# Layer 0's x1 turned by DMA, and another order of products in a turn

## The chip, the cores and the metric

The kernel runs on 1 core of one Trainium2 chip. The metric is device time in microseconds (us) of the whole program; lower is better. Engines are named as in the profile: PE is TensorE (matmuls), PEld its weight loads, DVE is VectorE, ACT is ScalarE, POOL is GpSimd and SP is SyncE, which issues the DMAs.

## What is computed

There are 128 graphs of 64 nodes with 768 features, float32 throughout, and two layers. Each layer is `x = layernorm(x + layer(x, adj))`. Layer 0 is a graph attention of 12 heads with a gate; layer 1 is a masked self-attention of 6 heads.

```python
def _L0_gnn_ref(feat_in, adj, W, b, w_src, w_dst, H_w, H_b):
    h = jnp.einsum('bnd,ade->bane', feat_in, W)
    th = jnp.tanh(h)
    attn_src = jnp.einsum('bane,aeo->bano', th, w_src)
    attn_dst = jnp.einsum('bane,aeo->bano', th, w_dst)
    attn = attn_src + jnp.swapaxes(attn_dst, 2, 3)
    attn = jnp.where(attn >= 0, attn, LEAKY_ALPHA * attn)
    attn = jnp.where(~adj[:, None, :, :], jnp.float32(-999.0), attn)
    attn = jax.nn.softmax(attn, axis=-1)
    feat_out = jnp.einsum('banm,bame->bane', attn, h) + b
    feat_out = jax.nn.elu(heads_joined(feat_out))
    gate = jax.nn.sigmoid(feat_in @ H_w.T + H_b)
    return gate * feat_out + (1.0 - gate) * feat_in

def _L1_gnn_ref(seq_inputs, Wq, bq, Wk, bk, Wv, bv, Wf, bf, graph_mask):
    q, k, v = (_heads(seq_inputs @ w + c) for w, c in ((Wq, bq), (Wk, bk), (Wv, bv)))
    scores = jnp.einsum('bhqd,bhkd->bhqk', q, k) / np.sqrt(HEAD_SIZE)
    probs = jax.nn.softmax(scores + bias, axis=-1)      # bias: 0 or -9e15 by the mask
    return heads_joined(jnp.einsum('bhqk,bhkd->bhqd', probs, v)) @ Wf + bf
```

(`heads_joined` is shorthand for the swap of axes and the reshape.)

## The kernel before

The 8192 rows are worked in 32 pairs; a pair is two tiles of 128 rows, called tile 0 and tile 1. Every dense product of a pair is done by a scheme of seven block products instead of eight, so a product of a pair (`h`, the gate `g`, the values `v`, the output `o`) is a `Job` of seven steps. A name such as `h5` is product 5 of the job `h`; it is six matmuls of 128x128 by 128x384 (L275). Products 1, 2 and 4 read blocks of the transposed input itself; 6, 5, 7 and 3 read sums of blocks (`block_sums`, L245 to L248): product 5 reads the first sum, 6 the second, 7 the third, 3 the fourth. A job keeps one PSUM bank `y` from product 1 to product 4 or so, a bank `x` for product 2 and a bank `z` for products 5 and 3. Banks of `x` and `z` share the tag `z`, with three buffers; `y` has three, and a tag `m` two. What a product left in PSUM is taken out by `way_out` one step later, after the next product has been issued: for `h` and `v` by an ACT copy or a DVE addition (L837 to L839, L866 to L868), for the gate by DVE (L853 to L855).

The schedule is written out by hand (`manual_schedule`): engines run their instructions in the order of the program. Layer 0 is a loop of turns. A turn walks through a list of products (`TURN` in most turns), and at each position of the list a set of acts is issued after the product. In turn p, `n0` and `n1` are the tiles of the new pair p, whose `h` and gate are made and whose attention weights are prepared; `t0` and `t1` are the tiles of the old pair q = p - 1, whose attention, gating and layernorm are finished, and whose layer-1 values `v` are begun. Products called `u` are the rest of the values of the pair before that; `G` and `H` are a gate left over or an `h` begun early. The acts that the text speaks of:

- new pair: `products` (L873: tanh on ACT, two multiplications by the attention vectors on DVE and POOL), `terms` (L881: a sum over 64 on DVE, then a store `dstd` and two loads `dd` that spread one of the terms over the partitions), `with_bias` (L893: POOL, and two loads `hx` of half of h), `logits` (L913, DVE), `leaky` (L923, ACT), `masked` (L929 to L936, DVE), `exps` (L942, ACT);
- old pair: `probs_by_nodes` (six PE transposes, bank m, two ACT copies into `pT`), `attend` (L974: 48 small matmuls `av` in two banks m), `features` (L990, L991 on DVE, L998 on ACT), `gate_tanh` (L1054, L1055, ACT), `residual` (L1004, POOL), `elu1` and `gated` (L1009 to L1016, DVE), `stats` and `normed` (the layernorm, L321 to L331; the result x1 is stored to DRAM);
- then `by_features`: x1 is transposed by PE, six transposes a tile into bank m (L953, `x1Tp`), and ACT copies them into `x1T` (L954). `v_begins` and `v_sums` make the operands of `v` from `x1T` on DVE; `spill_features` stores `x1T` for layer 1, `spill_values` stores the finished v;
- for the next pair: `load_xT` and `x_sums`, four sums on POOL. From turn 2 until it is done `sum_weights` also builds sums of layer-1 weights, with POOL operations (L366) and small DMAs, one step at each position.

All DMAs are issued on SP, in order. The pools give three buffers to `h`, to the gate and to the small tiles, five to `work`, two to `x1`, `v` and `x`, one to `x1T`, `pT` and the sums.

The list of a usual turn and of the last one, and the acts that by_features belongs to:

```python
TURN = [
    "h1", "h2", "u4", "u3", "h6", "g1", "h5", "h7", "g2", "g6", "h4",
    "h3", "g5", "g7", "v1", "v2", "g4", "v6", "g3", "v5", "v7",
]
            was(8, do(by_features, t1), do(stats, t0))
            was(9, do(normed, t0))
            was(12, do(v_begins))
            was(15, lambda: v_sums[q][0](), lambda: v_sums[q][1](), do(spill_features, q))
            at(11, new, do(products, n1))
            was(11, do(by_features, t0))
```

Layer 1 turns its attention weights by DMA already: `split` copies the 16-bit halves of the words apart (ACT, L574), `send` stores them to DRAM, `turn` brings each half back transposed with `dma_start_transpose` (L584), `join` puts the halves together (ACT, L591).

Of the kernel before, what the change touches and what calls it, by code (L numbers as in the profile page):

```python
# [62 lines left out]
    7.5: 12, 0: 7, 1: 7, 2: 8, 3: 9, 4: 10, 5: 11, 6: 12, 7: 12, 8: 13, 9: 14, 11: 15, 12: 15, 15: 16, 16: 17, 19: 19,  # L63
# [31 lines left out]
    ["u4", "u3"]  # L95
    + [f"q{n}" for n in (0, 1, 2, 3, 4, 5, 6, 8, 7, 9, 10, 11, 12)]
    + ["v1", "v2", "v6", "q13", "v5", "v7", "q14", "v4", "v3"]
)
LAST_AT = {7.5: 8, 3: 3, 4: 4, 5: 5, 6: 6, 7: 7, 8: 9, 9: 10, 11: 12, 12: 13, 15: 15, 16: 17, 19: 18}
# [27 lines left out]
    "h1", "h2", "u4", "u3", "h6", "g1", "h5", "h7", "g2", "g6", "h4",  # L127
    "h3", "g5", "g7", "v1", "v2", "g4", "v6", "g3", "v5", "v7",
]

THIRD_AT = {pos: max(int(pos) - 2, 0) for pos in [*range(len(TURN)), 7.5]}
TURNS = {
    0: (FIRST, FIRST_AT, {}),
    1: (SECOND, SECOND_AT, SECOND_OLD),
    2: (TURN[2:], THIRD_AT, THIRD_AT),
}


@with_exitstack
def kernel(  # L140
# [41 lines left out]
    x1T_d = [dram.tile([P, KC, PAIR * P], F32, name=f"x1Td_{p}") for p in range(NP)]  # L182
    v_d = [dram.tile([P, D], F32, name=f"vd_{t}") for t in range(2 * NP)]
    dst_d = [dram.tile([P, H0], F32, name=f"dstd_{t}") for t in range(2 * NP)]

    halves_d = [dram.tile([2, GT, P, P], U16, name=f"halvesd_{i}") for i in range(3)]
# [40 lines left out]
    def all_of(steps):  # L227
        for s in steps:
            s()

# [263 lines left out]
    class Attention:  # L494
# [81 lines left out]
        def send(self):  # L576
            nc.sync.dma_start(
                out=halves_d[self.f].rearrange("h i p c -> p h i c"),
                in_=self.halves(self.scT_, False).rearrange("p h (i c) -> p h i c", c=P),
            )  # L580

        def turn(self):
            for h in range(2):
                nc.sync.dma_start_transpose(  # L584
                    out=self.halves(self.flat, False)[:, h],
                    in_=halves_d[self.f][h].rearrange("i p c -> (i p) c"),
                )
# [155 lines left out]
    with ExitStack() as ph, ExitStack() as ph_r:  # L743
# [21 lines left out]
        def sums_of(eng, pool, tag, t, name):  # L765
            return block_sums(
                eng,
                sum_tiles(pool, tag, P, name),
                t[:, :HK, :P],
                t[:, HK:, :P],  # L770
                t[:, :HK, P:],
                t[:, HK:, P:],
            )
# [17 lines left out]
        A[0], x_steps = sums_of(G, sbr, "sx", xTs[0], "x0")  # L791
# [78 lines left out]

        def products(t):

            h = st[t]["h"]  # L873
            th = sbr.tile([P, 2, D], F32, tag="th", name=f"th_{t}")
            S.activation(th[:, 1, :].rearrange("p (a e) -> p a e", e=E0), h[:, :, :E0], AF.Tanh)  # L875
            V.tensor_tensor(th[:, 0, :], th[:, 1, :], wsd[:, 0, :], ALU.mult)  # L876
            G.tensor_tensor(th[:, 1, :], th[:, 1, :], wsd[:, 1, :], ALU.mult)  # L877
            st[t]["th"] = th

        def terms(t):  # L880
# [5 lines left out]
            nc.sync.dma_start(out=dst_d[t], in_=sd[:, :H0])  # L886
            dd = work(f"dd_{t}")
            for g in range(2):
                nc.sync.dma_start(
# [137 lines left out]
        x1Ts, B = {}, {}  # L1027

        def by_features(t):
# [4 lines left out]
            for half in range(2):  # L1034
# [4 lines left out]
                )  # L1039

# [29 lines left out]
        def value_sums(q):  # L1070
            B[q], v_sums[q] = sums_of(V, sb, "sv", x1Ts[q], f"v{q}")

        def x_sums(p):
            operands, steps = sums_of(G, sbr, "sx", xTs[p], f"x{p}")
            all_of(steps)
            A.setdefault(p, {}).update(operands)

        def third_begins():
            x = xTs[2]
            A[2] = {1: x[:, :HK, :P], 2: x[:, HK:, :P]}  # L1080
            jobs["H"] = h_job(2)
# [13 lines left out]
        for p in range(NP + 1):  # L1095
# [3 lines left out]
            if new:  # L1099
                jobs["G"] = jobs.get("g")  # L1100
                jobs["h"], jobs["g"] = jobs["H"] if p == 2 else h_job(p), gate_job(p)
            plan = {}

            turn, of_new, of_old = TURNS.get(p, (TURN, {}, {})) if new else (LAST, {}, LAST_AT)

            def at(pos, ok, *acts, places=of_new):
                if ok:
                    plan.setdefault(places.get(pos, int(pos)), []).extend(acts)

            def was(pos, *acts):  # L1110
                at(pos, old, *acts, places=of_old)
# [4 lines left out]
            def v_begins():  # L1116
                value_sums(q)
                jobs["v"] = v_job(q)


            was(0, do(probs_by_nodes, t1))
            at(0, old, do(exps, t0), do(gate_tanh, t1), places={0: 6} if p == 1 else of_old)
            was(1, do(residual, t1))
            was(2, do(attend, t1), do(gate_tanh, t0))
            was(3, do(features, t1), do(probs_by_nodes, t0), do(residual, t0))
            was(4, do(elu1, t1), do(gated, t1))
            was(5, do(attend, t0), do(stats, t1))
            was(6, do(features, t0), do(normed, t1))
            was(7, do(elu1, t0))
            was(7.5, do(gated, t0))  # L1130
            was(8, do(by_features, t1), do(stats, t0))
            was(9, do(normed, t0))
            was(12, do(v_begins))
            was(15, lambda: v_sums[q][0](), lambda: v_sums[q][1](), do(spill_features, q))
            was(16, lambda: v_sums[q][2]())
            was(19, lambda: v_sums[q][3]())

            at(0, p + 1 < NP, do(load_xT, p + 1))
            at(3, new, lambda: adjs.__setitem__(p, load_adj(sb, 2 * p, PAIR, f"adj_{p}")))
            at(6, new, do(mask, p))  # L1140
            at(4, 0 <= p - 2 < NP, do(spill_values, p - 2))
            at(8, new, do(inputs, p))
            at(11, new, do(products, n1))
            was(11, do(by_features, t0))
            at(12, new, do(products, n0))
            at(13, new, do(terms, n1), do(with_bias, n1))
            at(14, new, do(terms, n0), do(with_bias, n0))
            at(15, new, do(plus_one, p))
            at(16, new, do(logits, n1))
            at(17, new, do(leaky, n1))  # L1150
            at(17, p + 1 < NP, do(x_sums, p + 1), places={17: 12} if p == 0 else of_new)
            at(18, new, do(masked, n1), do(logits, n0))
            at(19, new, do(exps, n1), do(leaky, n0))
            at(20, new, do(masked, n0))

            if p == NP - 1:

                at(2, True, do(load_wide, "q", wq, range(4)))
                at(8, True, do(load_wide, "q", wq, range(4, 8)))
                at(12, True, do(load_wide, "q", wq, range(8, NW)))  # L1160
                at(9, True, do(load_wide, "k", wk, range(4)))
                at(15, True, do(load_wide, "k", wk, range(4, 8)))
                at(18, True, queries_begin)
                at(20, True, do(load_wide, "k", wk, range(8, NW)), lambda: jobs["rows"].ready(2))
            if p == NP:
                flush()
                for act in plan.pop(0):
                    act()
# [6 lines left out]
            if p == 1:  # L1175
                at(14, True, third_begins, places={})
# [161 lines left out]
```

## Time and profile before

| | |
|---|---|
| median of 3 runs | 2906.42 us (2904.89 to 2909.09) |
| profiled execution | 2904.88 us, of which the span of instructions is 2903.1 us |
| granted TensorE clock | 0.997 |
| PE, DVE, ACT, POOL busy | 99%, 66%, 37%, 35% of the span |
| layer 0 | up to about 1535 us of the span |
| x1 transposes on PE (x1Tp) | 384 matmuls, 52.5 us busy |

The profile is of one execution. A line of the groups reads: source line, engine, operation, written tile <- read tiles, shapes, count, then busy us and mean ns of one, then the idle time of the engine just before them with what ended it. A line of the timeline starts with the time from the span's start and the length. In the row of 40 slices each digit is the busy share in tenths. PE's matmuls overlap, so the distance from one start to the next counts, not the length. "q" behind an engine's name (SPq) is its queue of DMA issues.

### The profile page before, as it was taken

To read this page: it belongs to the slowest core of one execution; us is meant where nothing else is said; L and a number is where in the kernel's file an instruction comes from. 1 tells how busy PE (TensorE), PEld (TensorE's weight loads), DVE (VectorE), ACT (ScalarE), POOL (GpSimd) and SP (SyncE) were. 2 spreads that over 40 slices of the span, in tenths; PEclk is the share of its full clock that TensorE was granted. 3 is DMA by queue.
4 is the path that set the end of the run, shared out by engine and by line. 5 is a ranking of instruction groups with operands and counts; after the bars stand their busy time and mean duration, and the time that the engine had idled before them with its cause. 6 is when DMAs were issued, how large, how long until landed. Compare 5 with 4: busy or idle time off the path is not lost.

```text
span 2903.1 us, 45587 instructions
## 1 busy us (share of the span) xinstructions
PE 2860.5 (99%) x17676; PEld 1965.3 (68%) x17676; DVE 1930.0 (66%) x3045; ACT 1060.0 (37%) x1896; POOL 1022.1 (35%) x857
## 2 busy tenths in 40 slices
PE   7999999999999999999999999999999999999998
PEld 4565665566665665666668777877777877777885
DVE  6888788888878888788863654554564454565445
ACT  2344444444444444444433312333312333312232
POOL 2434354443444444343352323332223332123321
PEclk9999999999999999999999999999999999999999
DMA  5344444444434343333353323333223333223332
GB/s 175 123 139 135 138 137 131 138 131 143 147 126 146 125 146 127 105 113 110 117 198 108 108 84 100 105 99 103 65 82 100 103 102 100 74 75 101 99 88 73
DMA packets 307864, 335.20 MB, mean 115 GB/s; under 512 B 146241, under 2 KB 234305, under 8 KB 307649
## 3 DMA queue, kind: packets, MB, share of 16 engines
q1 hardware_dynamic: 307648, 332.29, 36.3%
q8 instruction: 140, 2.29, 0.3%
q14 instruction: 76, 0.61, 0.1%
HBM read 188.26 MB, written 119.14 MB: 106 GB/s over the span
## 4 chain that ended last, share of the span: by engine, by line
PE 84%; DVE 9%; ACT 2%; DMA 2%; issue 2%; POOL 1%; SPq 1%; POOLq 0%; DVEq 0%; ACTq 0%
PE y_o L275 9%; PE z_k L444 8%; PE z_q L444 8%; PE y_h L275 7%; PE y_g L275 6%; PE y_v L275 6%; PE y_k L444 5%; PE y_q L444 5%; PE z_o L275 4%; PE z_h L275 4%; PE z_v L275 3%; PE z_g L275 3%; PE x_o L275 2%; PE x_g L275 2%; PE sp L518 2%
## 5 line engine op out<-in xcount | busy, mean ns | idle before, releaser
L542 ACT ACTIVATE sc<-sc 128x512 f32<-128x512 f32 x48 | 30.2, 629 | 735.1 <-DVE sc L539 735.1
L327 POOL TENSOR_TENSOR rs_b<-ve_b,minus_half 128x1 f32<-128x1 f32 x64 | 35.2, 550 | 645.0 <-DVE ve_b L325 576.9
L444 PE MATMUL z_q<-xs,w_wq 128*128 128x256 f32 x896 | 213.5, 381 | 0.3 <-POOL xs L408 0.3
L672 POOL TENSOR_TENSOR y<-y,bf_bc 128x768 f32<-128x768 f32 x64 | 125.2, 1978 | 247.1 <-DMA y<-x1d 247.1
L444 PE MATMUL z_k<-xs,hw_wk 128*128 128x256 f32 x840 | 200.0, 381 | 0.0
L459 DVE TENSOR_TENSOR qT<-qT,z_q 128x512 f32<-128x512 f32 x96 | 65.8, 686 | 200.7 <-PE z_q L444 200.6
L1004 POOL TENSOR_TENSOR x<-gate,x 128x768 f32<-128x768 f32 x64 | 117.5, 1837 | 229.7 <-ACT gate L1055 214.9
L408 POOL TENSOR_TENSOR xs<-r,r 128x512 f32<-128x512 f32 x112 | 155.0, 1400 | 96.3 <-PE z_k L444 62.9
L444 PEld LDWEIGHTS z_q<-xs,w_wq 128*128 128x128 f32 x896 | 168.7, 190 | 24.3 <-POOL xs L408 0.7
L877 POOL TENSOR_TENSOR th<-th,wsd 128x768 f32<-128x768 f32 x64 | 117.3, 1833 | 164.9 <-DVE th L876 164.9
L444 PEld LDWEIGHTS z_k<-xs,hw_wk 128*128 128x128 f32 x840 | 158.4, 190 | 21.9
L696 DVE TENSOR_TENSOR y<-y_o,y 128x384 f32<-128x384 f32 x128 | 71.1, 556 | 132.8 <-PE y_o L275 132.7
L327 POOL TENSOR_TENSOR rs_a<-ve_a,minus_half 128x1 f32<-128x1 f32 x64 | 36.0, 562 | 340.7 <-DVE ve_a L325 340.7
L275 PE MATMUL y_h<-w_wq,xT 128*128 128x384 f32 x384 | 136.1, 491 | 8.2 <-DMA w_wq<-in_w_dram 7.6
L275 PE MATMUL y_v<-wv,sv_v 128*128 128x384 f32 x384 | 136.0, 490 | 5.1 <-DVE sv_v L246 4.5
L275 PE MATMUL y_h<-w_wq,sx_x 128*128 128x384 f32 x384 | 136.5, 492 | 4.2 <-ACT h L837 4.2
L275 PE MATMUL y_v<-wv,x1T 128*128 128x384 f32 x384 | 137.4, 495 | 1.8 <-ACT x1T L954 1.0
L275 PE MATMUL z_h<-w_wq,sx_x 128*128 128x384 f32 x384 | 137.6, 495 | 0.6 <-DVE w_wq L221 0.6
L275 PE MATMUL z_v<-wv,sv_v 128*128 128x384 f32 x384 | 137.8, 495 | 0.0
L275 PE MATMUL y_g<-hw_wk,sx_x 128*128 128x384 f32 x384 | 134.9, 488 | 2.5 <-DVE hw_wk L224 2.2
L876 DVE TENSOR_TENSOR th<-th,wsd 128x768 f32<-128x768 f32 x64 | 67.6, 1057 | 103.6 <-ACT th L875 103.6
L275 PE MATMUL z_g<-hw_wk,sx_x 128*128 128x384 f32 x384 | 134.4, 486 | 0.0
(181 smaller groups left out, 6718.3 us busy)
## 6 DMA issues: line engine op xcount, KB each, us to landing
x<-in_x_dram SPq DMA_DIRECT2D x64, 384.0 KB, 3.6
dd<-dstd SPq DMA_DIRECT2D x128, 192.0 KB, 3.4
x1d<-x SPq DMA_DIRECT2D x64, 384.0 KB, 2.6
x1Td<-x1T SPq DMA_DIRECT2D x32, 768.0 KB, 4.4
vd<-v SPq DMA_DIRECT2D x64, 384.0 KB, 2.9
r<-x1Td SPq DMA_DIRECT2D x96, 256.0 KB, 3.2
v<-vd SPq DMA_DIRECT2D x384, 64.0 KB, 2.3
y<-x1d SPq DMA_DIRECT2D x64, 384.0 KB, 5.8
```

The lines of the kernel that those rows point to most:

```text
L275: T.matmul(to[:, : self.n], lhsT, rhs, start=kc == 0 and not more, stop=kc == HK - 1, skip_group_check=more,)
L327: G.tensor_tensor(rstd, ve, minus_half, ALU.pow)
L408: G.tensor_tensor(t, self.of(x[0]), self.of(x[2]), x[1])
L444: T.matmul(b[:, half * W2 : (half + 1) * W2], w[:, kc, half * P : (half + 1) * P], x[:, kc, :], start=half == kc == 0 and not more, stop=k ...
L459: V.tensor_tensor(at, at, b.rearrange("p (h t) -> p h t", h=2), ALU.add if sign > 0 else ALU.subtract,)
L518: T.matmul(self.sp_[gr * N : (gr + 1) * N, (i * 2 + a) * N : (i * 2 + a + 1) * N], qT[:, 2 * self.f + a, at], kT[:, 2 * self.f + a, at], s ...
L542: S.activation(self.sc_, self.sc_, AF.Exp, scale=SCALE)
L672: G.tensor_tensor(y, y, pools["bf"], ALU.add)
L696: V.tensor_tensor(at(*mn), b, at(*mn), ALU.add)
L876: V.tensor_tensor(th[:, 0, :], th[:, 1, :], wsd[:, 0, :], ALU.mult)
L877: G.tensor_tensor(th[:, 1, :], th[:, 1, :], wsd[:, 1, :], ALU.mult)
L1004: G.tensor_tensor(xp, st[t]["gate"], xp, ALU.mult)
```

## The change

x1 of pairs 2 to 29 is no longer transposed by PE. `apart` copies the two 16-bit halves of its words apart (both halves on ACT for tile 0; one on POOL, one on ACT for tile 1), `send` stores them to DRAM, `turned` brings them back with six DMA transposes of 512 rows by 128 columns into the tile that later holds the value sums (`sv`), and `joined` puts the words together with four ACT copies into `x1T`. Pairs 0, 1, 30 and 31 keep the PE transposes.

The order of products changes in all turns from the third on. All seven value products of a pair now run as `u` in the next turn, spread over positions 1 to 13; products 1, 2, 6 and 5 of `h` of the next pair (`H`) run among the gate's at the end of the turn; `x_sums` of the next pair is issued in three parts at positions 13, 16 and 20. The acts are placed anew: `exps` of both new tiles and `probs_by_nodes` of n1 are now in the same turn as their logits, and `attend` of t1 comes at position 1. `products` and `terms` are cut into `tanh`, `products`, `terms` and `spread`. The third turn has a list of its own (`THIRD`), the last full turn another (`NO_NEXT`), and the closing one (`LAST`) takes 29 products instead of 24. The acts of the first two turns stay as they were, but for `gated` of t0 in the second, which is now asked for at 7 instead of 7.5 and lands at the same position.

The core of the diff (renamed DRAM tiles, moved helper arguments and the place tables of the edge turns are left out):

```diff
 LAST = (
-    ["u4", "u3"]
-    + [f"q{n}" for n in (0, 1, 2, 3, 4, 5, 6, 8, 7, 9, 10, 11, 12)]
-    + ["v1", "v2", "v6", "q13", "v5", "v7", "q14", "v4", "v3"]
+    ["u1", "u2", "u6", "q0", "u5", "q1", "q2", "u7", "q3", "q4", "u4", "u3"]
+    + [f"q{n}" for n in (5, 6, 8, 7, 9, 10, 11)]
+    + ["v1", "v2", "q12", "v6", "v5", "q13", "v7", "q14", "v4", "v3"]
 )
...
 TURN = [
-    "h1", "h2", "u4", "u3", "h6", "g1", "h5", "h7", "g2", "g6", "h4",
-    "h3", "g5", "g7", "v1", "v2", "g4", "v6", "g3", "v5", "v7",
+    "h7", "u1", "g1", "u2", "h4", "u6", "h3", "u5", "g2", "u7", "g6",
+    "g5", "u4", "u3", "H1", "g7", "H2", "H6", "H5", "g4", "g3",
 ]
...
+THIRD = [
+    "h6", "h5", "u4", "g1", "h7", "u3", "g2", "h4", "g6", "h3", "g5", "H1", "g7", "H2", "H6", "g4", "H5", "g3",
+]
...
+NO_NEXT = [
+    "h7", "g1", "u1", "h4", "u2", "h3", "u6", "g2", "u5", "g6", "u7", "g5", "u4", "g7", "u3", "g4", "g3",
+]
...
+    halves_d = [dram.tile([2, PAIR * P, D], U16, name=f"halvesd_{p}") for p in range(NP)]
...
+        def apart(t):
+            sp = work(f"sp_{t}").bitcast(U16).rearrange("p (two e) -> p two e", two=2)
+            x1 = words(st[t].pop("x1"))
+            if t % 2:
+                G.tensor_copy(sp[:, 0], x1[:, 0])
+            else:
+                S.copy(sp[:, 0], x1[:, 0])
+            S.copy(sp[:, 1], x1[:, 1])
+            st[t]["halves"] = sp
+
+        def send(t):
+            p, i = divmod(t, 2)
+            nc.sync.dma_start(
+                out=halves_d[p][:, i * P : (i + 1) * P, :].rearrange("h t d -> t h d"),
+                in_=st[t].pop("halves"),
+            )
+
+        def turned(p, *chunks):
+            if p not in sv:
+                sv[p] = sb.tile([P, 4, HK, P], F32, tag="sv", name=f"sv_{p}", bufs=1)
+            for c in chunks:
+                nc.sync.dma_start_transpose(
+                    out=landing(p)[:, c],
+                    in_=halves_d[p][:, :, c * P : (c + 1) * P].rearrange("h t f -> (h t) f"),
+                )
...
+        def joined(p):
+            x1Ts[p] = sb.tile([P, KC, PAIR * P], F32, tag="x1T", name=f"x1T_{p}", bufs=1)
+            dst = x1Ts[p].bitcast(U16).rearrange("p c (t two) -> p two c t", two=2)
+            land = landing(p).rearrange("p c (two t) -> p two c t", two=2)
+            for kh in range(2):
+                for half in range(2):
+                    rows = slice(kh * HK, (kh + 1) * HK)
+                    S.copy(dst[:, half, rows], land[:, half, rows])
...
+            by_pe = old and q in (0, 1, NP - 2, NP - 1)
+            by_dma = old and not by_pe
...
+            def of_turn():
...
+                at(0, p + 1 < NP, do(load_xT, p + 1), places={})
+                at(0, True, do(gate_tanh, t1), do(residual, t1))
+                at(1, True, do(attend, t1))
+                at(2, True, do(features, t1), do(probs_by_nodes, t0))
+                at(2, new, lambda: adjs.__setitem__(p, load_adj(sb, 2 * p, PAIR, f"adj_{p}")))
+                at(3, True, do(elu1, t1), do(gated, t1), do(gate_tanh, t0), do(residual, t0))
+                at(4, True, do(attend, t0), do(stats, t1))
+                at(5, True, do(features, t0), do(normed, t1))
+                at(5, new, do(mask, p))
+                at(6, True, do(elu1, t0), do(gated, t0))
+                at(6, by_dma, do(apart, t1))
...
+                at(7, True, do(stats, t0))
+                at(7, by_dma, do(send, t1))
+                at(7, new, do(tanh, n1), do(products, n1), do(inputs, p))
+                at(8, True, do(normed, t0))
+                at(9, by_dma, do(apart, t0))
+                at(10, by_dma, do(send, t0))
+                at(10, new, do(tanh, n0))
...
+                at(11, new, do(terms, n1), do(products, n0))
+                at(12, new, do(spread, n1))
+                at(13, new, do(terms, n0))
+                at(11, p + 1 < NP, do(next_begins, p + 1))
+                at(13, p + 1 < NP, do(x_sums, p + 1, 0))
+                at(14, new, do(spread, n0))
+                at(14, by_dma, do(turned, q, *range(KC)))
+                at(14, new, do(with_bias, n1), do(with_bias, n0), do(plus_one, p), do(logits, n1))
...
+                at(15, new, do(leaky, n1))
+                at(16, new, do(masked, n1), do(logits, n0))
+                at(16, True, do(spill_values, p - 2))
+                at(17, new, do(exps, n1))
+                at(18, new, do(leaky, n0), do(masked, n0))
+                at(18, by_dma, do(joined, q), do(v_begins))
+                at(16, p + 1 < NP, do(x_sums, p + 1, 1))
+                at(20, p + 1 < NP, do(x_sums, p + 1, 2))
+                at(19, by_dma, v_sum(0), v_sum(1), do(spill_features, q))
+                at(20, by_dma, v_sum(2))
+                at(21, by_dma, v_sum(3), places={21: len(turn)})
+                at(19, new, do(exps, n0))
+                at(20, new, do(probs_by_nodes, n1))
```

An act whose position lies past the end of the list is carried into the next turn. `H` is the job of the next pair's `h`, begun by `next_begins`.

## The prediction

> **What bounds the kernel now.** I read the page first, then the stretches between the first attention product of one pair and that of the next.
>
> ```profile
> span 2903.1 us, 45587 instructions
> PE 2860.5 (99%) x17676; PEld 1965.3 (68%) x17676; DVE 1930.0 (66%) x3045; ACT 1060.0 (37%) x1896; POOL 1022.1 (35%) x857
> PE   7999999999999999999999999999999999999998
> DVE  6888788888878888788863654554564454565445
> ```
>
> TensorE (PE) sets the time; layer 0 is the part with VectorE (DVE) at eight tenths. Two sums over whole turns:
>
> ```profile
> 153.50:1118.90 965.40, 959.95 (x5171) 581.67 (x5170) 784.60 (x1134) 420.46 (x674) 423.28 (x379) 1.00 0.42 137
> 1118.90:1438.10 319.20, 319.20 (x1725) 193.85 (x1725) 258.38 (x378) 140.12 (x225) 115.79 (x98) 1.00 0.36 114
> ```
>
> Columns are us, PE, PEld, DVE, ACT, POOL busy, clock, DMA share. The first is 21 turns of 45.97 us, in which `sum_weights` also runs on POOL and SP; the second is 7 turns of 45.60 us without it, with PE busy throughout. These 28 are exactly the pairs whose x1 goes through the DMA in the change. DVE is busy 36.9 of 45.6 us, ACT 20.0, POOL 16.5. So a turn shrinks only by taking work from PE, and only as far as DVE's and ACT's chains follow. What is taken away, on PE's timeline:
>
> ```profile
> 1176.98 2.10 PE L275 MATMUL x_g<-hw_wk,xT 128*128 128x384 f32 x6
> 1178.91 0.82 PE L953 MATMUL x1Tp<-ident,x 128*128 128x128 f32 x6
> 1179.57 2.10 PE L275 MATMUL y_g<-hw_wk,sx_x 128*128 128x384 f32 x6
> ```
>
> A product holds PE for 1.93 us (1178.91 - 1176.98), six transposes for 0.66 (1179.57 - 1178.91). Prices of what replaces them stand in layer 1, which already transposes by DMA (issues, groups, and the SP queue):
>
> ```profile
> dd<-dstd SPq DMA_DIRECT2D x128, 192.0 KB, 3.4
> sc<-halvesd SPq DMA_TRANSPOSE x90, 2.5
> L591 ACT COPY scT<-sc 128x512 uint16<-128x512 uint16 x90 | 62.9, 771 | 7.2 <-DMA sc<-halvesd 7.2
> L574 ACT COPY scT<-sc 128x512 uint16<-128x512 uint16 x90 | 50.7, 611 | 4.9 <-issue 4.9
> L584 SPq DMA_TRANSPOSE sc<-halvesd x90: 1122/1242/2142, 1575.5 to 2789.7; - x90
> ```
>
> **The change, part by part.**
>
> *PE.* 28 pairs lose 2 x 0.66 us: 1.31 us a turn, 36.8 us. The products are the same, only moved.
>
> *ACT.* Lost: four copies of 0.48 us a pair. Added: three `apart` copies and four `joined` copies of 768 16-bit elements, 1.5 times those of L574 and L591: at most 0.92 and 1.16 us. ACT goes from 20.0 to about 25.5 of 44 us. The four `joined` copies stand in a row, at most 4.6 us; I take 3.7, because in layer 1 the second copy starts 0.62 us after the first, before its end.
>
> *POOL.* One `apart` copy of the odd tile, between 0.9 us (ACT's) and 1.8 (POOL's 128x768 operations). It meets `gated` of the even tile on DVE. L246 on DVE took 0.56 us with POOL idle and 1.23 beside it, so I bound the loss by 0 and 0.9 us; it falls before a stretch in which DVE has some 1.5 us idle, so I take 0. The Trainium skill, "SBUF — State Buffer", Who interferes with whom, says that a DVE instruction with two SBUF inputs contends with a GpSimd one that reads SBUF and that the loser blocks fully. By it the loss could be the copy's whole 1.8 us, 0.3 a turn beyond the idle time, 8 us in all; the rows show a part of that.
>
> *SP and DMA.* Two sends and six transposes a turn: 6 x 1.24 = 7.4 us of SP's queue, behind them the `hx` loads, the v stores and the next xT. The hx loads land near 20.7 on the clock used below, wanted at 23.9; the v stores, moved from position 4 to 16, near 24, just when u1's result wants their buffer, but ACT waits there anyway (see the new wait). So nothing for these. Traffic grows by 1.6 MB on the 5.2 MB of a turn (114 GB/s x 45.6 us); the DMA share of 0.36 to 0.42 stays under 0.6. One issue turns 512x128 elements, four blocks of 128x128, so SP's 1.24 us are 0.31 a block. The skill's "VectorE: DVE Perf Modes", Rules for kernel authors, speaks against the change: transpose 128x128 on TensorE where PSUM will do (390 ns in bf16, against 1309 by the crossbar). By it, as an estimate, the 28 x 12 x 2 blocks of 16-bit halves would take 880 us on the DMA against PE's 37, were they on the path; no row here shows 1309 ns a block.
>
> *Does it arrive late?* I lay one turn out by hand. Zero is PE's start of g5 (position 11). `terms` of n1 (1.74) ends at 2.4; its store and the two `dd` loads have landed 5.4 later (in the trace the store is issued at 1190.39, the second load at 1192.35, landing 3.5 after that), so `logits` starts at 7.9; with POOL beside it, 2.2 us (L913: 1.50 to 2.65). Then two g7 results, `masked` n1 (3.1), `logits` n0 (1.5), H2's result, 0.4 waiting for `leaky`, `masked` n0 (3.1): DVE is through at 19.6. SP has sent the second `dd` at 9.6 and issues transposes from there until 17.1; the last lands near 18.5. `joined` starts at 16.5 after `leaky` n0 and, its second half waiting for that landing, ends at 20.2; the value sums follow, 0.55 each with POOL idle (the shortest of L245 to L248), and the next turn's head results by 24. ACT does exps n0 and both pT copies by 21.6. PE, five products, six transposes and two products after position 16 (9.7), wants pT for `attend` t1 at 23.9. Slack: 2.3 us. POOL meanwhile does n0's product until 5.3, the first two x sums until 7.9 (wanted by H6 at 11.6), `with_bias` until 11.3, the third sum until 12.6 (wanted by h7 at 20.0) and the fourth after g3.
>
> *The new wait.* There are three h buffers. H1's result, at position 15, takes the third, so h7's result at position 1 must wait until `attend` t1 has read the oldest. POOL's memset, ACT's copy (0.46), DVE's addition (0.55) and `features` (1.48) follow `attend` by 2.6 us in all; on PE only g1 (1.94) and half the transposes of probabilities (0.33) stand between. The second half waits some 0.3 to 0.45 us. In the trace of before this wait (pTp on DVE fo) is 1.6 us over all 28 turns. Queued behind it on ACT are u1's result and `features`' exponential, both wanted later. The z and y banks, followed through the new order, are released a product or more ahead.
>
> *Sum.* Late turns: 45.60 - 1.31 + 0.45 = 44.74. Turns with `sum_weights`: they lose 0.37 now (3.0 us of it the value sums' wait, which goes), and the same POOL and SP intrusions meet a tighter chain; between 0 and 1.0, I take 0.45: 45.2. Gain 21 x 0.77 + 7 x 0.86 = 22.2 us.
>
> *The edges.* The third turn has 18 products for 19, the last full one 17 for 21, the closing one 29 for 24. The first two are then shorter on PE (about 39 and 38 us) than DVE's chain (36.9 busy, and at least 3 of waits): together 2 to 6 us lost. The closing turn has more filler, and the 2.95 us that PE idles in the one window from 1438.1 to 1489.1 may shrink: 0 to 3 regained. Net I take 3 lost, bounds -3 and +6.
>
> The profiled execution took 2904.88 us (span 2903.1), the median of the runs is 1.5 above it. 2904.9 - 22.2 + 3 + 1.5 = 2887 us.
>
> **The rivals.**
>
> *All covered.* No new stall, and the 8 us of old ones (21 x 0.37) go too: 2906.4 - 36.8 - 8 + 3 = 2865, without the latter 2873. For: PE has no wait in the 7 late turns now. Against: three h buffers.
>
> *DVE becomes the bound.* DVE's 8.7 us of idle time a turn are then latency, not slack: the loop terms, store, load, logits, masked, sums, features, stats, products stays near 45.5, whatever PE does. Time 2903 to 2910, no change. For: 36.9 us busy in 44.7 is 83%. Against: the walk leaves DVE about 1.5 us idle before each g5 result.
>
> *Slower: `joined` blocks ACT.* Place: position 18, the ACT queue, with exps n0, both pT copies and the gate's tanh behind it. It decides once the last transpose lands 2.3 us later than laid out; from there each us is a us of PE in each of 28 turns, so at 3.0 us later the 19 us are gone (28 x 0.7). Layer 1's issue row reaches 2.14 us instead of 1.24: if six ran at that, the landing is 5.4 us later and the time 2887 + 28 x 3.1 = 2974; at 4 us, 2935. For: dd also gates the transposes, since SP takes them in order. Against: the row's median is 1.24. Source rows here lie 1,536 B apart, which no row of the trace prices.
>
> **How the numbers follow.** The forecast 0.56 (2874 to 2900: 21 turns by 0.45 less or 0.55 more are 9 and 12 us, the edges 6 less or 3 more, not all at once); all covered 0.12; DVE bound 0.12; `joined` late 0.20. A measurement of this kernel can tell about 0.2%, 5.8 us, from no change. Faster by more: the first two and a part of the third, 0.74. Within: 0.08. Slower: most of the last, 0.18. The range leaves out half of "all covered" and most of the slower case: 2866 to 2916.
>
> **What would show it.** PE's time on x1Tp falls from 52.5 us to 4/32 of it, 6.6. Late turns take 44.5 to 45.0 us. A wait of PE on DVE fo or rden for pTp, 0.3 to 0.45 us a turn, 8 to 13 us in all, behind a wait of the h copy or memset for `av`. DVE busy about 37 us a turn, in 44.7. Wrong would be: turns at 45.5 or more with PE waiting for pT or av (ACT late), ACT waiting over 2 us a turn on the landing of sv, or PE waiting on the value sums.

## The result and the profile after

The changed kernel takes 2951.89 us (median of 4 runs, 2951.39 to 2957.31) against 2906.32 us before: a ratio of 1.0158, 95% interval 1.0146 to 1.0171. It is 1.6% slower, where 2887 us was forecast. PE has indeed lost work: 17340 matmuls for 17676, and the 384 transposes of x1 are 48. But it is no longer busy throughout layer 0. The page of the changed kernel:

```profile
span 2950.6 us, 45305 instructions
...
PE 2849.9 (97%) x17340; PEld 1940.5 (66%) x17340; DVE 1909.6 (65%) x3045; ACT 1177.4 (40%) x1980; POOL 1078.8 (37%) x885
...
PE   7899999999999999999989999999999999999998
...
DVE  6777877777787777777763645545654554554445
```

The same two stretches of turns as before the change, the 21 with `sum_weights` and the 7 behind them:

```profile
158.70:1154.60 995.90, 949.16 (x4915) 560.18 (x4914) 771.90 (x1130) 507.22 (x735) 465.55 (x400) 0.99 0.55 163
1154.60:1473.50 318.90, 312.66 (x1642) 186.14 (x1642) 248.63 (x381) 169.86 (x247) 131.16 (x105) 1.00 0.49 150
```

A turn now takes 47.42 us in the first and 45.56 in the second. PE is busy for 45.20 and 44.67 us of it, so the work was taken away and waits took its place. The execution profiled is 47.5 us longer in its span. By place, from attention product to attention product:

| part | forecast | measured | missed by |
|---|---|---|---|
| 21 turns with `sum_weights` | -16.2 (21 x 0.77) | +30.5 | 46.7 |
| 7 late turns | -6.0 (7 x 0.86) | -0.3 | 5.7 |
| edges: start +0.8, third turn +4.4, closing turn +7.0, first products of layer 1 +5.1 | +3 | +17.3 | 14.3 |

What PE waits for, over the whole program (us in total, times, longest):

```profile
PE y_v L290 <- ACT v L881: 24.8, 12, 6.6
PE pTp L978 <- DVE rden L1015: 19.2, 28, 1.7
PE av L999 <- ACT pT L979: 10.8, 14, 1.9
...
PE y_g L290 <- DVE gate L868: 4.4, 1, 4.4
```

Only the second was in the forecast (8 to 13 us; 24.5 here with a row of 5.3 us on DVE fo). The first and the third say that ACT is late, the last is one wait in the third turn.

### The profile page after: what moved, and what is told of

It reads as the page before. It is cut to its first block, busy times and chain, and to the rows that moved or that the text cites. A ratio compares the mean times of both kernels' runs of the same rounds, so it can differ in the third digit from the quotient of the medians.

```text
span 2950.6 us, 45305 instructions
## 1 busy us (share of the span) xinstructions
PE 2849.9 (97%) x17340; PEld 1940.5 (66%) x17340; DVE 1909.6 (65%) x3045; ACT 1177.4 (40%) x1980; POOL 1078.8 (37%) x885
## 4 chain that ended last, share of the span: by engine, by line
PE 67%; DVE 11%; SPq 6%; issue 5%; DMA 4%; ACT 4%; POOL 2%; ACTq 0%; POOLq 0%; DVEq 0%
PE y_o L290 8%; PE z_q L459 8%; PE z_k L459 8%; PE y_q L459 5%; PE y_k L459 5%; SPq L1089 5%; PE y_v L290 4%; PE z_o L290 4%; PE y_h L290 3%; PE y_g L290 3%; PE z_v L290 3%; PE x_o L290 2%; DMA sv<-halvesd 2%; PE sp L533 2%; DVE fo L1016 2%
## 5 line engine op out<-in xcount | busy, mean ns | idle before, releaser
L1029 POOL TENSOR_TENSOR x<-gate,x 128x768 f32<-128x768 f32 x64 | 131.0, 2046 | 169.3 <-ACT gate L1122 158.1
L459 PEld LDWEIGHTS z_q<-xs,w_wq 128*128 128x128 f32 x896 | 168.8, 190 | 24.5 <-issue 0.5
L902 DVE TENSOR_REDUCE sd<-th 128x24 f32<-128x1536 f32 x64 | 111.9, 1748 | 59.3 <-POOL th L896 59.3
L290 PE MATMUL y_v<-wv,sv 128*128 128x384 f32 x384 | 139.2, 499 | 6.7 <-ACT v L881 6.6
L290 PE MATMUL y_g<-hw_wk,xT 128*128 128x384 f32 x384 | 139.0, 499 | 4.4 <-DVE gate L868 4.4
L938 DVE TENSOR_TENSOR att<-dd,sd 128x768 f32<-128x768 f32 x64 | 117.8, 1841 | 36.8 <-DMA dd<-dstd 36.6
L290 PE MATMUL z_v<-wv,sv 128*128 128x384 f32 x384 | 137.2, 494 | 0.0
```

Of the source, the lines that this page charges most:

```text
L290: T.matmul(to[:, : self.n], lhsT, rhs, start=kc == 0 and not more, stop=kc == HK - 1, skip_group_check=more,)
L459: T.matmul(b[:, half * W2 : (half + 1) * W2], w[:, kc, half * P : (half + 1) * P], x[:, kc, :], start=half == kc == 0 and not more, stop=k ...
L902: V.tensor_reduce(sd, th.rearrange("p s (a e) -> p (s a) e", e=E0), AX.X, ALU.add)
L938: V.tensor_tensor(att3, dd.rearrange("p (m a) -> p a m", a=H0), sd[:, H0:].unsqueeze(2).to_broadcast([P, H0, N]), ALU.add,)
L1029: G.tensor_tensor(xp, st[t]["gate"], xp, ALU.mult)
```

## Experiments

**What is order, what is DMA, what is `sum_weights`.** Four kernels came first: the new order with x1 still turned by PE; the sums left out of the changed kernel and of the one before; and the changed kernel with the sums' DMAs but without their additions.

```diff
# e1: every pair by PE
-            by_pe = old and q in (0, 1, NP - 2, NP - 1)
+            by_pe = old
# e2, e3: sum_weights stores one plain block and adds nothing
-                    acc = pool.tile(...) ... G.tensor_tensor(acc, acc, t, ...)
+                    nc.sync.dma_start(out=wide_d[key][n][:, kc, :], in_=block(*blocks[0][:2]))
# e7: loads and stores stay
-                        G.tensor_tensor(acc, acc, t, ALU.add if sign > 0 else ALU.subtract)
```

> The new order of products with x1 of every pair turned by PE as before (by_features of t1 and t0 at positions 12 and 13, v_begins at 14). It separates the order from the DMA turn. Theory 1: the late turns are held by a chain that the DMA turn makes: ACT takes u7's result out only after the layernorm and the two apart copies of tile 0, DVE idles 2.6 us for it, so terms, dd, the six transposes and joined come some 2 us later than laid out, and with them the gate's tanh, h7's copy, features and the transposes of probabilities. Then without it a late turn takes 45.5 to 45.7 us with no wait of PE, the first 21 turns 45.9 to 46.3, and the whole about 2952 - 21 x 1.3 = 2925. Rival: the order itself stalls (h7's copy waits for a buffer until attend of t1 has read it): PE still waits 0.8 us for pTp in each turn and pays the transposes on top: late turns 46.5 or more, the whole 2965 or more.

> The changed kernel without sum_weights' sums: each wide_d half gets the first plain block by one DMA, spread over the same turns; the loads, the POOL operations and so the values of layer 1 are left out. Theory 1: the loads of sum_weights queue behind the six transposes on SP, its POOL operation waits for them and holds up residual and the layernorm, which then collide with gated on DVE; without it turns 2 to 22 fall from 47.4 to the late turns' 45.6, that is 21 x 1.8 = 38 us: 2914. Rival: those turns are long for another reason (DMA traffic of the early part, the clock after gaps), and stay above 47: 2945 or more.

> The kernel before with the same left out (the sums of layer 1's weights). Both theories: its turns 2 to 22 fall from 45.97 to 45.6, 8 us: 2898. It is the base for the run without sums of the changed kernel; the difference of the two is what DMA turn and order cost without sum_weights: theory 1 says 15 to 18 us, all of it in the third turn, the last turns and layer 1's first group.

> The changed kernel with sum_weights' DMAs all kept and its POOL additions left out (layer 1's weights are then wrong). Theory 1: POOL no longer waits for loads that stand behind the transposes, so turns 2 to 22 fall to 45.6 to 46.0: 2952 - 32 = 2920 or less. Rival: it is the DMAs on SP between the stores and loads of dd, or the traffic, that lengthen these turns: they stay at 47 or more, 2945 or more.

| kernel | median us | ratio to before, interval | a turn of 21, us | a late turn, us |
|---|---|---|---|---|
| before | 2906.3 | 1 | 45.97 | 45.60 |
| changed | 2951.9 | 1.0158 (1.0146 to 1.0171) | 47.42 | 45.56 |
| e1, order alone | 2939.7 | 1.0115 (1.0085 to 1.0144) | 46.78 | 46.04 |
| e2, changed, no sums | 2906.7 | 1.0001 (0.9990 to 1.0012) | 45.38 | 45.3 |
| e3, before, no sums | 2899.6 | 0.9976 (0.9965 to 0.9988) | 45.61 | 45.6 |
| e7, changed, no additions | 2907.0 | 1.0007 (0.9996 to 1.0018) | 45.46 | 45.2 |

Three things follow. Without sums the change is 7 us slower than the kernel before without them (15 to 18 had been expected): its 28 turns win 0.2 to 0.3 us each of the 1.3 that PE was relieved of, 7 us in all, and its edges lose twice that. The sums, which cost 6.7 us before, cost 45 after, and e7 shows that it is not their traffic. And the order by itself already costs 33 us, between the two theories' numbers for e1: it carries both edge waits (5.25 us in the third turn, 7.26 in the closing one) and 17 us in the 21 turns. Its 21 turns are 0.83 us longer than its last six late turns (45.95), against 0.37 in the kernel before, though no transposes stand in SP's queue there. So a part of what the sums cost came with the new order alone.

**The late turns: u7 behind the layernorm.** In these turns DVE stood idle for 2.61 us just before u7's addition. DVE and ACT of the changed kernel in one late turn (start, length, in brackets the idle time before):

```profile
1265.24 0.21 DVE L345 TENSOR_SCALAR sh_a<-mv_a,rs_a 128x1 f32<-128x1 f32 x1 [0.44 <-POOL rs_a L342]
1265.38 0.55 DVE L869 TENSOR_TENSOR gate<-x_g,gate 128x384 f32<-128x384 f32 x1
1268.53 0.56 DVE L882 TENSOR_TENSOR v<-z_v,v 128x384 f32<-128x384 f32 x1 [2.61 <-ACT v L881]
```

```profile
1265.49 1.03 ACT L346 ACTIVATE x<-x,sh_a,rs_a 128x768 f32<-128x768 f32 x1 [4.23 <-DVE sh_a L345]
1266.56 0.83 ACT L1073 COPY sp<-x 128x768 uint16<-128x768 uint16 x1
1267.29 0.83 ACT L1074 COPY sp<-x 128x768 uint16<-128x768 uint16 x1
1268.03 0.47 ACT L881 COPY v<-y_v 128x384 f32<-128x384 f32 x1
```

ACT first waits for the layernorm of t0, then copies x1 apart, and only then takes out u7 (L881), on which DVE's addition and all behind it wait: `terms`, `dd`, the transposes, `joined`. Two edits test it, one by one and together: u7 and n0's tanh ahead of `apart` of tile 0, and no `apart` copy on POOL (there it stretched `gated` of t0, L1039, from 0.96 to 1.59 us).

```diff
# e4 (e6 has both)
-                at(9, by_dma, do(apart, t0))
-                at(10, by_dma, do(send, t0))
                 at(10, new, do(tanh, n0))
+                at(10, by_dma, do(apart, t0))
+                at(11, by_dma, do(send, t0))
# e5
-            if t % 2:
-                G.tensor_copy(sp[:, 0], x1[:, 0])
-            else:
-                S.copy(sp[:, 0], x1[:, 0])
+            S.copy(sp[:, 0], x1[:, 0])
```

> The changed kernel with two acts swapped: tanh of n0 and, by its place, the taking out of u7 on ACT come ahead of apart of tile 0, whose copies and store follow one position later. Theory (ACT takes u7's result out only after it has waited for the layernorm of t0 and copied x1 apart, so DVE's addition of u7, terms, dd, transposes and joined all come some 2 us late): DVE's 2.6 us idle before L882 in a late turn shrinks to under 1 us, the seven late turns fall from 45.56 to 44.8 (44.6 to 45.1), and the whole to 2925 to 2940. Rival (the third h buffer or DVE's chain holds the turn, whatever ACT's order is): late turns within 0.2 us of 45.56 and the whole within 6 us of 2952. Second rival (apart, one position later, delays the transposes by as much as terms gain): late turns 45.5 to 46.

> The changed kernel with both apart copies on ACT also for tile 1, none on POOL. Theory (POOL's copy of 16-bit words beside gated of t0 on DVE, L1039 1.59 us against 0.96 alone, is a part of the delay): L1039 of t0 back to 1.0 us, late turns 45.56 to 45.0 or 45.3, whole 2936 to 2946. Rival (ACT is the engine that is late, so 0.7 us more on it in each turn cost more than DVE wins): late turns 45.6 to 46.1, whole 2952 to 2968.

> Both edits: u7 taken out ahead of apart of tile 0, and no apart copy on POOL. Theory (two parts of one delay on the way to dd and the transposes): late turns 44.4 to 44.9, which is PE without a wait at 44.3; whole 2915 to 2935. Rival (h buffer or DVE's chain): late turns stay at 45.3 to 45.6.

The first gave 2927.8 us (1.0071, 1.0056 to 1.0086), the second 2929.4 (1.0076, 1.0061 to 1.0091), both 2907.4 (1.0002, 0.9992 to 1.0012): 24, 22.5 and 44.5 us less than the changed kernel, so the two nearly add up. The second and both together came out below their ranges, by 7 and 8 us. In e4 the idle time before the addition is 1.00 us:

```profile
1249.70 0.46 ACT L881 COPY v<-y_v 128x384 f32<-128x384 f32 x1
```

```profile
1250.19 0.56 DVE L882 TENSOR_TENSOR v<-z_v,v 128x384 f32<-128x384 f32 x1 [1.00 <-ACT v L881]
```

and the last six late turns take 44.5 to 44.6 us each, with 0.17 us of waits. That settles the late turns: neither the h buffers nor DVE's busy time hold them. Most of what the second edit gained came in the 21 turns (46.58 us each, from 47.42); why so much there was not tried.

**The 21 turns: POOL behind SP's queue.** One such turn of the changed kernel. SP's issues, the ones of the sums last:

```profile
528.58 1.08 SPq L914 DMA_DIRECT2D dd<-dstd  x2
529.76 7.73 SPq L1089 DMA_TRANSPOSE sv<-halvesd  x6
...
540.08 0.60 SPq L390 DMA_DIRECT2D wided_q<-wacc_q  x1
540.78 0.87 SPq L1135 DMA_DIRECT2D vd<-v  x2
542.13 0.89 SPq L374 DMA_DIRECT2D wacc_q<-in_wq_dram  x1
543.07 0.46 SPq L377 DMA_DIRECT2D wadd_q<-in_wq_dram  x1
```

POOL, whose next addition waits for that load, with `residual` (L1029) behind it:

```profile
546.61 0.73 POOL L381 TENSOR_TENSOR wacc_q<-wacc_q,wadd_q 128x256 f32<-128x256 f32 x1 [7.83 <-DMA wadd_q<-in_wq_dram]
547.30 1.82 POOL L1029 TENSOR_TENSOR x<-gate,x 128x768 f32<-128x768 f32 x1
549.06 0.12 POOL L833 MEMSET h<- 128x24 f32 x1
549.53 0.99 POOL L381 TENSOR_TENSOR wacc_q<-wacc_q,wadd_q 128x256 f32<-128x256 f32 x1 [0.36 <-DMA wadd_q<-in_wq_dram]
550.48 2.52 POOL L1029 TENSOR_TENSOR x<-gate,x 128x768 f32<-128x768 f32 x1
```

and DVE's `elu1` and `gated`, which these then meet:

```profile
547.82 2.11 DVE L1034 SCALAR_TENSOR_TENSOR ex<-ex,fo 128x768 f32<-128x768 f32 x1 [0.54 <-ACT ex L1023]
549.96 1.37 DVE L1039 SCALAR_TENSOR_TENSOR ex<-gate,ex 128x768 f32<-128x768 f32 x1
551.43 2.38 DVE L1041 TENSOR_TENSOR x<-ex,x 128x768 f32<-128x768 f32 x1
```

The three take 5.86 us, for 2.88 at the same place of a late turn. From there the layernorm, `apart` and u7's copy are late. Three experiments tried to take the waiting away. e8 steps `sum_weights` only at positions 2 to 12, ahead of the transposes. e11 issues only its loads on ACT's queue. e14 keeps the additions but loads once, so that none waits.

```diff
# e8, with one of the three or two yields of each wait less
-                if 2 <= p < NP - 1:
+                if 2 <= p < NP - 1 and 2 <= pos <= 12:
# e11
-                        nc.sync.dma_start(out=t, in_=block(k, f))      # and acc
+                        nc.scalar.dma_start(out=t, in_=block(k, f))    # and acc
# e14: acc and t are made and loaded ahead of the loops; the stores send t
-                        nc.sync.dma_start(out=t, in_=block(k, f))      # and acc
```

> The changed kernel with the steps of sum_weights only at positions 2 to 12 of a turn, ahead of the six transposes, with one step less of each wait, so that all of them still fit before turn 30. Same loads, sums and stores. Theory (the loads stand behind the transposes in SP's queue and POOL, which works in order, waits for them into the next turn's residual, which then runs beside gated on DVE): POOL's waits on wadd and wacc shrink to a third or less, turns 2 to 22 fall from 47.4 to between 45.4 and 46.2, and the whole to 2910 to 2930. Rival (it is the 2.3 us of POOL's additions themselves a turn, beside DVE's instructions, wherever they stand): turns stay at 46.8 or more, whole over 2938.

> The changed kernel with one edit: the loads of sum_weights (wacc, wadd) are issued on ACT's queue instead of SP's, at the same positions; the sums on POOL and the stores stay. Theory (the loads stand behind the six transposes and the hx, v and xT issues on SP, and POOL's next addition holds up residual): POOL no longer idles 7 to 12 us at the end of a turn before L381, gated on DVE (L1034, L1039, L1041) is stretched less, turns 2 to 22 fall from 47.4 to 45.6 to 46.4, whole 2915 to 2932. Rival (POOL's additions beside DVE cost it wherever their data come from, or the issues delay ACT, which is itself late in the turn): turns 46.8 or more, whole over 2940.

> The changed kernel in which sum_weights loads its two tiles once and then only repeats the 88 additions and 48 stores at the same places (the stores take the tile that is never written; the sums of layer 1's weights are left out, so q and k are wrong). No addition waits for a load, and the store waits for none. Theory (it is POOL waiting for loads that stand behind the transposes, not its additions): turns 2 to 22 at 45.4 to 45.9, as without the additions (45.45), whole 2907 to 2918. Rival (the additions themselves, 2.3 us of POOL a turn beside DVE): 46.6 or more, whole 2932 or more. Between the two, each has its share.

e8 gave 2928.8 us (1.0076, 1.0061 to 1.0091) with 46.5 us a turn: the whole lies in its range, but a turn won only half of what was hoped for. PE's waits for u4's bank (y_v) are nearly gone, those for pT (`av`) are not.

e11 went the wrong way: 2994.7 us (1.0307, 1.0291 to 1.0323). It moved the wait, not the cause. There is one `wacc` buffer, so ACT must hold the next load back until SP has issued the store (at 203.64, landing 2.03 later), behind the transposes:

```profile
205.74 0.33 ACTq L374 DMA_DIRECT2D wacc_q<-in_wq_dram  x1
206.16 0.54 ACTq L377 DMA_DIRECT2D wadd_q<-in_wq_dram  x1
206.75 0.48 ACT L852 COPY h<-y_h 128x384 f32<-128x384 f32 x1 [8.99 <-issue]
```

Here ACT stands still for 8.99 us, and PE for 5.61 at its next product. The rival had named ACT's issues, and the numbers are the rival's; of POOL's additions e11 says nothing. e14 does: 2910.7 us (1.0014, 1.0005 to 1.0023), 45.67 us a turn. All 88 additions, none waiting, cost 0.2 us a turn more than none at all (e7, 45.46, which has all the loads too); their waits cost 1.75. Its 21 turns:

```profile
156.30:1115.40 959.10, 939.56 (x4915) 559.73 (x4914) 752.85 (x1132) 507.13 (x735) 467.48 (x400) 1.00 0.50 152
```

POOL's waits for the loads of q's sums over the stretch, before, changed and in the last experiment (e15, below):

```profile
POOL wacc_q L366 <- DMA wadd_q<-in_wq_dram: 36.7, 13, 4.3
```

```profile
POOL wacc_q L381 <- DMA wadd_q<-in_wq_dram: 86.1, 13, 12.2
```

```profile
POOL wacc_q L381 <- DMA wadd_q<-in_wq_dram: 11.8, 4, 3.9
```

**The edges: the v stores.** In the closing turn PE waits 6.56 us at u6, because ACT can't write u1 before the v stores have landed, and SP issues those behind six loads of rows:

```profile
1508.35 3.54 SPq L441 DMA_DIRECT2D r<-x1Td  x6
1511.94 0.90 SPq L1135 DMA_DIRECT2D vd<-v  x2
```

```profile
1518.03 0.48 ACT L881 COPY v<-y_v 128x384 f32<-128x384 f32 x1 [4.84 <-DMA vd<-v]
```

```profile
1518.56 2.92 PE L290 MATMUL y_v<-wv,sv 128*128 128x384 f32 x4 [6.56 <-ACT v L881]
```

e9 issues the stores one position earlier in the last full turn, ahead of those loads, and puts the value sums of the third turn behind the gate's results.

```diff
+                if p == NP - 1:
+                    at(15, True, do(spill_values, p - 2), places={})
+                else:
+                    at(16, True, do(spill_values, p - 2))
...
-                at(14, by_pe, v_sum(0), v_sum(1), do(spill_features, q))
+                third = 4 * (p == 2)
+                at(14 + third, by_pe, v_sum(0), v_sum(1), do(spill_features, q))
...
```

> The changed kernel with two edits in edge turns only. In the last full turn the v stores of the pair before (spill_values) are issued at position 15 instead of 16, which puts them ahead of the six loads of rows for layer 1; in the third turn the value sums go four positions later (spill_features with them), behind the gate's results on DVE. Theory (u6 of the closing turn waits 6.5 us because ACT can't take out u1 until the v stores have landed, and g1's bank in the third turn is held up by two value sums of 2 us each that POOL stretches): the wait of y_v falls from 6.6 to about 2 us, that of y_g from 4.4 to 0.5 to 1.5 us, and the whole to 2941 to 2946. Rival (ACT's exponentials hold u1 up, not the stores; DVE is late in the third turn as a whole): both waits within 1 us of what they were, whole 2950 to 2954.

It gave 2939.8 us (1.0113, 1.0099 to 1.0126), 12 less. The two waits are 1.62 and 0.4 us, about as the theory had it, and the whole is 1 us below its range. By place, in the profiled executions, the third turn wins 4.8 us, the closing one 4.7, layer 1 2.7 and the late turns 1.6; the start and the 21 turns lose 1.7. The u6 product of e9:

```profile
1508.93 1.24 PE L290 MATMUL y_v<-wv,sv 128*128 128x384 f32 x3 [1.62 <-ACT v L881]
```

**All together.** e10 has the edits of e6, e8 and e9; e12 those of e6 and e9; e13 adds to e12 the loads on ACT's queue; e15 adds to e12 all DMAs of the sums on ACT's queue, stores too, and one position between an addition and the next load.

```diff
# e15 against e12
-                    nc.sync.dma_start(out=acc, in_=block(*blocks[0][:2]))      # and t, and the store
+                    nc.scalar.dma_start(out=acc, in_=block(*blocks[0][:2]))    # and t, and the store
                         G.tensor_tensor(acc, acc, t, ALU.add if sign > 0 else ALU.subtract)
+                        yield
```

> All remedies together: u7 taken out ahead of apart of tile 0, no apart copy on POOL, the steps of sum_weights at positions 2 to 12 only, and the two edits of the edge turns. Theory (the causes are separate, each with its own time): late turns 44.5 to 44.6, turns 2 to 22 at 44.6 to 45.3 (in the kernel without the last two remedies they take 45.8), edges 7 to 9 us less, whole 2880 to 2895, thus faster than before by 0.4 to 0.9%. Rival (once one is gone the next delay takes its place): no more than 8 us below the 2907 of the kernel with the first two, 2899 or more.

> u7 ahead of apart of tile 0, no apart copy on POOL and the two edits of the edge turns; sum_weights as in the changed kernel. Theory (separate causes add up: 2907.4 with the first two, edges worth 4.5 and about 4 us): 2896 to 2902, faster than before by 0.15 to 0.4%; late turns 44.5 to 44.6, turns 2 to 22 at 45.8. Rival (the edges' gain is swallowed by layer 1's start, which waits for loads): 2904 or more.

> The same with the loads of sum_weights on ACT's queue too. Theory: turns 2 to 22 fall from 45.8 to 44.7 to 45.1, whole 2874 to 2890, faster than before by 0.6 to 1.1%. Rival (POOL's additions themselves, or ACT's issues): turns 45.5 or more, whole 2892 or more.

> The kernel with u7 first, no apart copy on POOL and the edge edits (2898.8 us), and all DMAs of sum_weights, loads and stores, issued on ACT's queue, with one more position between an addition and the next load, so that no DMA of it stands behind the transposes on SP. Theory (place in SP's queue): turns 2 to 22 fall from 45.8 to 44.8 to 45.3, whole 2878 to 2890. Rival (ACT, which works in order, now waits for POOL's additions and for the landing of the stores before it can issue, as it did for 9 us in the kernel with the loads alone there): 2905 or more, with PE waiting on ACT or POOL h in turns of 47 us or more.

| kernel | median us | ratio to before, interval | a turn of 21, us |
|---|---|---|---|
| e10 | 2905.3 | 0.9994 (0.9985 to 1.0003) | 45.93 |
| e12 | 2898.8 | 0.9973 (0.9964 to 0.9982) | 45.76 |
| e13 | 2949.3 | 1.0152 (1.0138 to 1.0166) | 48.16 |
| e15 | 2886.4 | 0.9933 (0.9917 to 0.9950) | 45.13 |

e10 missed its range and came out as its rival said: with u7 out of the way, e8's edit costs 0.2 us a turn instead of winning 0.9. Why is not settled: over the 21 turns ACT waits about as long for the last transposes in both (18.9 us in e10, 17.7 in e12), but e10's profile has three stretches of 3.4 us at half clock there and e12's has one (see the last section). e13 repeats e11's failure (there 49.6 us a turn). e15 is faster than both kernels: 20 us below before, 65 below the change. Against e13 it changes two things at once, the queue of the stores and the one position more; which of them counts was not tried. Its two stretches:

```profile
151.70:1099.40 947.70, 934.85 (x4914) 557.02 (x4914) 734.27 (x1135) 523.34 (x759) 432.09 (x365) 1.00 0.57 169
1099.40:1412.80 313.40, 310.94 (x1639) 185.55 (x1638) 243.67 (x378) 174.36 (x253) 137.60 (x112) 1.00 0.54 163
```

## Why the prediction was wrong

*PE's gain was right.* The 28 pairs lost their transposes, and an undisturbed late turn takes 44.54 us (e4, e6, e12), for 44.74 forecast. 45.60 less 1.31 is 44.29; of the 0.25 above that, 0.17 is PE's wait for `features` (pTp on DVE fo), and the new order itself costs PE the rest (the last six late turns of e1, with the transposes, have the same wait and take 45.95).

*The walk by hand left out one step, and that step took most of its slack.* It has `terms` end at 2.4, as if u7's addition on DVE were ready when its product is; in the code that addition goes onto what ACT has copied out before it, and ACT was behind the layernorm and `apart`. Times since PE's start of g5:

| step | laid out | changed | e4 |
|---|---|---|---|
| `terms` of n1 ends | 2.4 | 3.9 | 2.4 |
| SP starts the transposes | 9.6 | 11.1 | 9.8 |
| the last one has landed | 18.5 | 20.3 | 19.0 |
| `joined` ends | 20.2 | 22.4 | 21.1 |
| `attend` of t1 | 23.9 | 24.0 | 24.0 |

With the step out of the way the walk holds within 0.9 us. With it, 2.2 of the 2.3 us of slack are gone, and the waits behind `attend` (pTp on DVE rden, 4.4 us in the 7 late turns, and av on pT, 1.7) are about the 5.9 us that e4 wins there.

*The term for `sum_weights` was the large error.* The text took 0.45 us a turn, bounds 0 to 1.0, for "the same POOL and SP intrusions meet a tighter chain". They were not the same: the loads had moved behind 7.7 us of transposes, and by e1 the new order made them dearer even without transposes in the queue. The forecast named what stands behind the transposes on SP as the `hx` loads, the v stores and the next xT, and left the sums' loads out, and with them POOL, which waits in order. Against 45.2 the turns took 47.42; 1.75 of the 2.2 us go when the additions don't wait (e14), and 1.65 when u7 and `apart` don't pass the delay on (e6). Together that is more than there is to win, as with two links of one chain; with both cut (e15) the turn is at 45.13.

*`apart` on POOL was taken at 0, with 0 to 0.9 as bounds.* The copy took 0.82 us and cost `gated` 0.63 us in a late turn, within the bounds; but the stretch behind it had no idle time to give, for the chain through ACT passed there (e5 wins 0.54 us a late turn). The two meet so:

```profile
1259.48 0.82 POOL L1071 COPY sp<-x 128x768 uint16<-128x768 uint16 x1 [2.71 <-ACT x L346]
```

```profile
1259.53 1.59 DVE L1039 SCALAR_TENSOR_TENSOR ex<-gate,ex 128x768 f32<-128x768 f32 x1
```

The copy ends 0.77 us after `gated` began. In the turn at 547 us shown above, `elu1` (L1034) began 1.30 us before the end of a `residual` on POOL and took 1.15 us longer than 0.96; L1039 began 0.56 us before the end of an addition and lost 0.41; L1041 began 1.57 us before the end of the other `residual` and lost 1.42. So each lost what POOL still had to do, less about 0.15 us. By the Trainium skill ("SBUF — State Buffer", Who interferes with whom) the port that the two share is an exclusive lock; this trace agrees with it. The forecast drew on the same rule for a copy of up to 1.8 us; the copy took 0.82.

*The edges were 3 us forecast and 17.3 measured.* The v stores had been put at nothing because ACT waits there anyway; in the closing turn that cover is gone. Third turn: 4.4 us against 2 to 6 for both edge turns. The 5.1 us in the first products of layer 1 were not tried; no other profile shows even half of them. Behind the last addition of v, the changed kernel's takes 1375.6 us, the one before 1370.5, those of the experiments 1370.4 to 1372.8.

*The rivals.* The slower one had the right place (position 18, ACT behind the last landing) and the wrong cause: the transposes were issued at 1.26 us each (median, for 1.24 expected) and landed in 2.9 us (median; 2.6 to 4.9), but they started late. DVE is not the bound: it is busy 35.5 us a late turn. The h-buffer wait, the forecast's own new wait, is 0.17 us where 0.45 was taken. e15 lands on 2886 us for the 2887 forecast, and its turns win 17.7 and 5.8 us for 16.2 and 6.0: the forecast described a kernel in which these waits had been seen to. That it is so close is partly luck, since the 0.45 for `sum_weights` was picked from between 0 and 1.0.

## What to carry to other kernels

When a long block of issues is put into an in-order queue, list everything that is issued behind it in the program, small background transfers first, and for each the engine that waits for it and what that engine has queued behind. In a walk by hand, follow each result to the engine that takes it out and ask what stands ahead of it there; a step that adds onto another engine's copy has two owners. Moving a transfer to another engine's queue moves its waits too: here it helped only when load and store went together and with one position more between, which were not tried apart.

## What the hardware showed beyond that

A pause of PE can cost more than its length. In the closing turn PE paused from 1512.0 to 1518.6 us, and the granted clock was 0.50 from 1515.3 to 1522.1, so for half of that time behind the pause. After a pause of 2.16 us in layer 1, which ended at 1661.2, it was 0.50 for 3.4 us. The length of a pause alone does not decide it: in the 21 turns of the changed kernel, pauses of 1.88, 1.96 and 2.60 us were followed by such a stretch (at 327.5, 617.6 and 231.9 us), pauses of 2.09 and 2.23 us (ended at 568.1 and 519.9) were not. Columns as above, the clock third from the end:

```profile
520.00:523.40 3.40, 3.40 (x11) 2.08 (x12) 3.40 (x4) 1.85 (x4) 0.00 (x0) 1.00 0.67 210
...
1515.30:1522.10 6.80, 3.54 (x6) 2.03 (x7) 2.50 (x2) 1.22 (x2) 5.52 (x4) 0.50 1.05 394
...
1662.10:1665.50 3.40, 3.40 (x10) 2.69 (x9) 3.40 (x5) 0.00 (x0) 3.40 (x3) 0.50 0.26 75
```

The Trainium skill, "TensorE: Matmul & The Clock Gate", Part 1, gives half rate after an idle window of about 3.4 us; the length of these stretches agrees with that window, but here pauses shorter than it were at times enough. Six matmuls of a product that fell into such a stretch took up to 4.21 us instead of 2.10 (e6's closing turn). As an estimate from that, a stretch of 3.4 us costs up to 1.7 us beyond the wait that a row shows, and the three in the 21 turns up to 5 of their 30 us.
